# Routing one-hots with pairs of token tiles innermost: one change to a four-block network on one NeuronCore

## The chip, the cores and the metric

The kernel runs on one core of a Trainium2 chip. A core has a matrix engine (TensorE, in the profile PE, with its weight loads as PEld), a vector engine (VectorE, DVE), an activation engine (ScalarE, ACT), a general engine (GpSimd, POOL) and an engine that here only issues DMAs (SyncE, SP). They share the on-chip memory SBUF (128 partitions); TensorE writes to PSUM. Each engine works through its own instructions in order and waits on semaphores for the others. The metric is the device time of one execution in microseconds; the median of several executions counts.

## The reference

The network takes 32 sequences of 256 tokens with 256 features and adds four residual blocks: modulated projection and cosine attention, adapter with attention and a mixture of experts, a second modulated projection with a feature-map attention, and embeddings with a butterfly feed-forward part. The change lies in the mixture of experts, cut here to what matters (T = 8192 tokens, 8 experts, C = 2048 places in each):

```python
logits = x @ wr
top1 = argmax(softmax(logits)); top2 = argmax(logits without top1)
loc1 = cumsum(m1, axis=0) - 1                      # m1, m2: one-hots of top1, top2
loc2 = cumsum(m2, axis=0) - 1 + m1.sum(0)
s1, s2 = loc1[tok, top1], loc2[tok, top2]          # C where the place is past the end
buf[top1, s1] = x; buf[top2, s2] = x               # tokens to places
h = relu(einsum('ecd,edf->ecf', buf, w1) + b1)
y = (einsum('ecf,efd->ecd', h, w2) + b2) * 0.8
out = g1 * y[top1, s1] + g2 * y[top2, s2]          # g: gates
```

To gather the tokens of an expert, the kernel needs the inverse of (expert, place): for each of the 8 x 2048 = 16384 places, the number of the token that sits there.

## The kernel before

The program has two stages, each planned as a whole. The first ("attention stage") runs 32 sequences through both attentions, up to the routing logits `L_all`; the second starts with routing, and goes on with the experts, the butterflies (products of weight matrices on VectorE), and the last two blocks.

**How the order is set.** Work is written as Python generators, `Part`s, which yield an engine and an estimated length before they emit instructions. The function `side_by_side` (L88) is a planner: it keeps a time for each engine, and lets the part go next that can start first. The order in which it emits is the order in each engine's queue on the chip. Buffers come from rings (`ring`, `get`, `back`): a part that wants a buffer of a ring whose turns are all taken waits in the plan too. Thus a different estimate, or a buffer from another ring, can change the written order of everything planned in the same stage. In the attention stage the ring `hp` has 3 buffers of 8 KB a partition, which the first attention's head softmax (L490 to L543) uses for its products; the ring `sh` has 12 of 2 KB. A ring `sc` with one buffer carries the attention scores from TensorE (L716) to ScalarE's exponential (L725, `pt`) in chunks, 8 a sequence.

**Constants.** The part `numbers` (L377) is planned with the attention stage, last in its list, and starts with `yield None, 300.0`, a delay in the plan. It makes the tables that routing needs: `i8b` (the numbers 0 to 127, each repeated), `prow` (the partition's number), `ttb` (the token tile's number), and masks. Its first temporary, `io`, is a buffer of the ring `hp`; the turn is taken when the part is first called, which is before the delay has passed.

**Routing** (L1042). Tokens lie as 64 tiles (NT) of 128 partitions. For each choice k (first, second) VectorE finds the expert (`m`), TensorE counts with a triangular matrix (`loc`, L1090 to L1100) the tokens before each one, and VectorE makes from that a slot number, expert times 2048 plus place, split into `hi` (slot / 128, NHI = 128 values) and `lo` (slot mod 128). The inverse is then computed by products of one-hots. For 8 tiles at a time (AT1), and both choices, that is 16 groups:

- VectorE makes `o1` (L1158: is hi equal to h, for 128 values h and 8 tiles), `ol` (L1161: is lo equal to l, for 128 values l) and the first half of `oh` (L1164: `o1` times the tile's number). All are bf16 with 1024 elements a partition. These three are planned as one step, `DVE2`[...].
- ScalarE makes the second half of `oh` (L1144: `o1` times the partition's number, `prow`).
- TensorE multiplies, for each tile i, `ol[:, :, i]` as weights with `oh[:, :, :, i]` as moving operand (L1135: 128 x 128 by 128 x 256), and sums all 128 products in `tps`: the tile's number and the partition's number of the token at each slot.

In each of these tiles the token tile i is the innermost index, of 8. What one product reads, of weights or of the moving operand, therefore lies 8 bf16 elements, 16 bytes, apart.

After the last product VectorE copies (`tf`, L1172) and combines (`tok`, L1173). GpSimd gathers the experts' tokens by `tok` (L1314), and the expert blocks start: transposes, `bh` (L1358), `by` (L1373), scatter (L1281). The butterflies' VectorE instructions (L1415 to L1421) are planned beside all this. In L1415 and L1419 one operand is a coefficient of a 2 x 2 matrix, taken out of a tile of f32 quadruples.

Of the kernel before, what the change touches and what calls it, by code (L numbers as in the profile page):

```python
# [15 lines left out]
I32 = mybir.dt.int32  # L16
AF = mybir.ActivationFunctionType
ALU = mybir.AluOpType
# [4 lines left out]
P = 128  # L23
# [9 lines left out]
PE, DVE, ACT, POOL, SP = "PE", "DVE", "ACT", "POOL", "SP"  # L33
# [3 lines left out]
BF = mybir.dt.bfloat16  # L37
# [129 lines left out]
def network(ctx: ExitStack, tc: tile.TileContext, a: dict, out: bass.AP):  # L167
    nc = tc.nc
# [5 lines left out]
    NHI = NSL // P  # L174
# [4 lines left out]
    cst = ctx.enter_context(tc.tile_pool(name="cst", bufs=1))  # L179
# [92 lines left out]
    def get(r, name, shape=None, dtype=F):  # L272

        pool, own, turns = rings[r]
        yield turns
        return pool.tile(shape or own, dtype, name=name, tag=r)

    def back(r):
        return "back", rings[r][2]
# [43 lines left out]
    with tc.tile_pool(name="sp", bufs=2) as sp, tc.tile_pool(name="spp", bufs=2, space=PSUM) as spp:  # L323
        wT["c"] = load_w(sp, "cwT", D)
        for l in ("k", "o", "c"):
# [5 lines left out]
            for m in range(2):  # L331
                nc.scalar.activation(
                    sty[l][:, m, :], ps[:, m, :], AF.Identity, bias=col(l + "aff", m),
                    scale=1.0 / math.sqrt(P) if l == "c" else 1.0,
# [18 lines left out]
        for n, o, w in (("dgb", 0, 2 * HID), ("ugb", 2 * HID, 2 * D)):  # L353
            g = sp.tile([P, w], F, name=n)
# [8 lines left out]
    SLAB = P // NE  # L363
    NSB = -(-NT // SLAB)
    AT1 = 8
    i8b = cst.tile([P, P, AT1], BF, name="i8b")
    prow = cst.tile([P, 1], F, name="prow")
    none = cst.tile([P, 1], F, name="none")
    place = cst.tile([P, CAP // P], F, name="place")
    ttb = cst.tile([P, NT], BF, name="ttb")  # L370
# [5 lines left out]

    def numbers():  # L377
        yield None, 300.0
        io = yield from get("hp", "io", [P, P, AT1], I32)
        yield POOL, 1.5  # L380
        nc.gpsimd.iota(io, [[1, P], [0, AT1]], base=0, channel_multiplier=0)
        yield ACT, 1.1
        nc.scalar.copy(i8b, io)
        yield DVE, 0.2
        nc.vector.tensor_scalar(rev, io[:, :NE, 0], -1.0, float(NE), ALU.mult, ALU.add)
        yield back("hp")
        io = yield from get("sh", "io", [P, 2, P], I32)
        yield POOL, 0.3
        nc.gpsimd.iota(io[:, 0, :NT], [[1, NT]], base=0, channel_multiplier=0)
        nc.gpsimd.iota(io[:, 1, :1], [[1, 1]], base=0, channel_multiplier=1)  # L390
        yield ACT, 0.5
        nc.scalar.copy(ttb, io[:, 0, :NT])
        nc.scalar.copy(prow, io[:, 1, :1])
        nc.scalar.activation(none, io[:, 1, :1], AF.Copy, bias=float(T))

        yield POOL, 1.0
        nc.gpsimd.memset(oneb, 1.0)
        nc.gpsimd.affine_select(
            utb, oneb.to_broadcast([P, P]), [[1, P]], ALU.is_ge, 0.0, base=0, channel_multiplier=-1
        )  # L400
        nc.gpsimd.iota(io[:, 0, :NE], [[-1, NE]], base=P, channel_multiplier=1)
        yield DVE, 0.4
        nc.vector.tensor_single_scalar(io[:, 0, :NE], io[:, 0, :NE], NE - 1, ALU.bitwise_and)
        nc.vector.tensor_scalar(e8b, io[:, 0, :NE], 0.0, None, ALU.is_equal)
        nc.gpsimd.iota(io[:, 1, : CAP // P], [[P, CAP // P]], base=0, channel_multiplier=1)
        yield ACT, 0.3
        nc.scalar.copy(place, io[:, 1, : CAP // P])
        yield back("sh")

        for n in range(NSB):  # L410
            yield POOL, 1.2
            nc.gpsimd.affine_select(
                before[:, n, :], e8b.unsqueeze(1).to_broadcast(W3),
                [[NE, NT], [1, NE]], ALU.is_gt, 0.0, base=-P * n, channel_multiplier=-1,
            )
# [548 lines left out]
    with tc.manual_schedule():  # L964
        side_by_side([*(Part(sequence(b, False)) for b in range(B)), Part(numbers())])
# [76 lines left out]
    def routing():  # L1042
# [28 lines left out]
        v_, hi_, lo_, cnt = [], [], [], []  # L1071
        for k in range(2):
# [5 lines left out]
            for n in range(NSB):  # L1078
                w = min(SLAB, NT - n * SLAB) * NE
# [4 lines left out]
            for n in range(NSB):  # L1084
                w = min(SLAB, NT - n * SLAB) * NE
# [5 lines left out]
            for n in range(NSB):  # L1091
                w = min(SLAB, NT - n * SLAB) * NE
# [4 lines left out]
            if k == 1:  # L1097
                for n in range(NSB):
                    w = min(SLAB, NT - n * SLAB) * NE
# [29 lines left out]
        tps = yield from get("mm", "tps", [P, 2, NHI])  # L1129
        last = None  # L1130

        def product(ol, oh, n, w):
            yield PE, 0.12 * w
            for i in range(w):
                nc.tensor.matmul(  # L1135
                    tps.rearrange("p a h -> p (a h)"), ol[:, :, i], oh[:, :, :, i].rearrange("p a h -> p (a h)"),
                    start=(n == 0 and i == 0), stop=(n == 2 * NT - w and i == w - 1),
                )
            yield back("sh")
            yield back("big")  # L1140

        def by_place(ol, oh, o1, n, w, before):
            yield ACT, 1.1
            nc.scalar.activation(oh[:, 1, :, :], o1, AF.Copy, scale=prow)  # L1144
            yield back("sh")
            if before is not None:
                yield "join", before
            yield from product(ol, oh, n, w)

        for k in range(2):  # L1150
            for t0 in range(0, NT, AT1):
                w = min(AT1, NT - t0)
                ol = yield from get("sh", "ol", [P, P, w], BF)
                o1 = yield from get("sh", "o1", [P, NHI, w], BF)
                oh = yield from get("big", "oh", [P, 2, NHI, w], BF)
                OB = [P, P, w]
                yield DVE2, 2.1
                nc.vector.tensor_tensor(  # L1158
                    o1, i8b[:, :NHI, :w], hi_[k][:, t0 : t0 + w].unsqueeze(1).to_broadcast([P, NHI, w]), ALU.is_equal
                )  # L1160
                nc.vector.tensor_tensor(  # L1161
                    ol, i8b[:, :, :w], lo_[k][:, t0 : t0 + w].unsqueeze(1).to_broadcast(OB), ALU.is_equal
                )
                nc.vector.tensor_tensor(  # L1164
                    oh[:, 0, :, :], o1, ttb[:, t0 : t0 + w].unsqueeze(1).to_broadcast([P, NHI, w]), ALU.mult
                )
                last = Part(by_place(ol, oh, o1, k * NT + t0, w, last))
                yield last
        yield "join", last
# [675 lines left out]
    def answer_out(b, begin, before):  # L1845
# [163 lines left out]
        yield "back", lanes_d  # L2009

    routed = Part(routing())
    loads, blocks = [], []
    for e in range(NE):
        w = {}
# [138 lines left out]
```

## Time and profile before

| | |
|---|---|
| median of 3 runs | 3989.45 us (3988.71 to 3994.0) |
| the profiled execution | 3993.62 us |
| its span | 3991.9 us |
| PE busy | 3627.3 us, 91% |
| weight loads | 2607.7 us, 65% |
| VectorE busy | 2471.0 us, 62% |
| ScalarE busy | 1787.2 us, 45% |
| GpSimd busy | 1979.5 us, 50% |
| first one-hot to `tok` | 1853.5 to 1914.6 us |

In the profile an instruction group reads: line, engine, operation, output<-input by the program's names, partitions x elements and type, count. Busy matmul time is pipelined time; a matmul's duration includes its drain, so that the time from one to the next is the busy time divided by the count. A wait line reads: who waited, for whom, microseconds in total, times, longest. The stage times in the busy-time view show the attention stage until about 1830 us, routing until about 1915 us, the experts with the butterflies until about 2850 us, then the last blocks. The granted TensorE clock is 0.50 of the full one from 1850 to 1915 us, and 1.00 from 1940 us on.

### The profile page before, as it was taken

Reading aid. Unit: us, or ns where it says so; the run is one execution under the profiler, and the core shown is the slowest. Engines: PE = TensorE matmul, PEld = TensorE weight load, DVE = VectorE, ACT = ScalarE, POOL = GpSimd, SP = SyncE. Lnnn points to the kernel's source line nnn. Section 1 sums busy time; section 2 is a strip of 40 time slices with the busy share of each in tenths; the row PEclk is TensorE's granted clock in tenths of the full one; section 3 lists DMA queues with packets and bytes.
Section 4 is the critical chain, followed back from the end, with each engine's and each line's share of the span. In section 5 each row is a group of like instructions: output and inputs, shape, how many; then the busy total and the mean of one; then the engine's idle time right before and its main releaser. Section 6 shows DMA issues by size and latency. Waiting matters only on the chain. (4 is left out here: it accounts for less than half of the span.)

```text
span 3991.9 us, 55591 instructions
## 1 busy us (share of the span) xinstructions
PE 3627.3 (91%) x21868; PEld 2607.7 (65%) x21869; DVE 2471.0 (62%) x3951; ACT 1787.2 (45%) x2682; POOL 1979.5 (50%) x1959
## 2 busy tenths in 40 slices
PE   2689898899999999887999999999898999999999
PEld 2356556566666666552566666666686888888888
DVE  6886898898999999625766452000236464565654
ACT  1367666667777777662222222222222333333333
POOL 4554445545555555420644656554215455565653
PEclk7699999999999999995899999999998999999999
DMA  1001000000000000002233433322242323232331
GB/s 63 5 16 32 22 24 15 26 26 26 26 26 26 27 28 26 23 18 90 74 99 91 106 88 85 62 47 48 67 157 77 104 83 104 88 116 87 100 102 43
DMA packets 134368, 237.17 MB, mean 59 GB/s; under 512 B 19249, under 2 KB 80817, under 8 KB 131538
## 3 DMA queue, kind: packets, MB, share of 16 engines
q0 software_dynamic: 48128, 100.77, 10.4%
q1 hardware_dynamic: 85826, 132.25, 9.9%
q8 instruction: 174, 2.85, 0.3%
q14 instruction: 96, 0.79, 0.1%
q10 hardware_dynamic: 144, 0.52, 0.0%
HBM read 182.99 MB, written 50.48 MB: 58 GB/s over the span
## 5 line engine op out<-in xcount | busy, mean ns | idle before, releaser
L725 ACT ACTIVATE pt<-sc 128x2048 f32<-128x2048 f32 x256 | 480.7, 1878 | 204.1 <-PE sc L716 202.0
L1373 PE MATMUL by<-w,hid 128*128 128x256 f32 x2048 | 452.7, 379 | 2.5 <-DVE ysb L1379 2.5
L1358 PE MATMUL bh<-ehT,w 128*128 128x512 f32 x1024 | 452.3, 595 | 1.5 <-ACT ehT L1327 1.5
L1347 ACT ACTIVATE hid<-bh,cols 128x512 f32<-128x512 f32 x256 | 174.8, 688 | 593.1 <-PE bh L1358 548.2
L1373 PEld LDWEIGHTS by<-w,hid 128*128 128x128 f32 x2048 | 386.5, 190 | 66.3 <-issue 13.9
L210 POOL TENSOR_TENSOR n<-n,negh 128x32 f32<-128x32 f32 x64 | 374.1, 5846 | 5.3
L1281 POOL DMA_INDIRECT rrows<-ysb,row x128 | 223.3, 1745 | 260.5 <-DMA rrows<-ysb,row 139.6
L698 PE MATMUL av<-pt,vaug 128*32 128x256 f32 x4096 | 292.0, 405 | 58.7 <-ACT pt L725 56.5
L1358 PEld LDWEIGHTS bh<-ehT,w 128*128 128x128 f32 x1024 | 194.9, 191 | 222.1 <-issue 215.9
L1379 DVE TENSOR_TENSOR ysb<-by,b 128x512 f32<-128x512 f32 x64 | 44.0, 688 | 454.4 <-PE by L1373 333.3
L716 PE MATMUL sc<-qT,kT 32*128 32x256 f32 x4096 | 306.1, 414 | 19.9 <-ACT pt L725 18.7
L539 DVE TENSOR_TENSOR hprod<-hprod 128x1024 f32<-128x1024 f32 (+2 forms) x384 | 317.0, 825 | 7.1
L531 DVE TENSOR_TENSOR hprod<-hex,kk 128x2048 f32<-128x2048 f32 x128 | 298.5, 2332 | 0.0
L716 PEld LDWEIGHTS sc<-qT,kT 32*128 32x128 f32 x4096 | 192.4, 192 | 131.4 <-issue 66.2
L1314 POOL DMA_INDIRECT xg<-h2buf,tok x128 | 150.3, 1174 | 211.5 <-DVE tok L1173 90.3
L1983 PE MATMUL dh<-zT,w_eff 128*128 128x256 f32 x1024 | 238.8, 383 | 5.7 <-DVE zT L1960 5.7
L698 PEld LDWEIGHTS av<-pt,vaug 128*32 128x32 f32 x4096 | 110.6, 113 | 188.1 <-ACT pt L725 86.3
L1997 PE MATMUL do<-w_con,gT 128*128 128x256 f32 x1024 | 231.7, 380 | 0.0
L1983 PEld LDWEIGHTS dh<-zT,w_eff 128*128 128x128 f32 x1024 | 191.2, 192 | 30.7 <-DVE zT L1960 6.9
L1997 PEld LDWEIGHTS do<-w_con,gT 128*128 128x128 f32 x1024 | 193.4, 191 | 25.4
L503 POOL COPY hex<-hex 128x30 f32<-128x30 f32 (+6 forms) x224 | 53.2, 237 | 308.8 <-ACT hex L518 308.8
L208 POOL TENSOR_SCALAR rstd<-mv 128x2 f32<-128x2 f32 x160 | 44.0, 275 | 317.8 <-DVE mv L307 309.9
(612 smaller groups left out, 7585.6 us busy)
## 6 DMA issues: line engine op xcount, KB each, us to landing
w<-in_w SPq DMA_DIRECT2D x16, 1024.0 KB
x<-rrows SPq DMA_DIRECT2D x64, 256.0 KB
bfw<-in_upw SPq DMA_DIRECT2D x10, 1024.0 KB
bfw<-in_dnw SPq DMA_DIRECT2D x10, 1024.0 KB
xT<-in_xT SPq DMA_DIRECT2D x32, 256.0 KB
x<-in_x SPq DMA_DIRECT2D x32, 256.0 KB
h2buf<-xh SPq DMA_DIRECT2D x32, 256.0 KB
ytbuf<-yT SPq DMA_DIRECT2D x32, 256.0 KB
```

Of the source, the lines that this page charges most:

```text
L210: nc.gpsimd.tensor_tensor(o, o, negh[:p].to_broadcast([p, n]), ALU.pow)
L531: nc.vector.tensor_tensor(pr.rearrange("p j (h d) -> p j h d", d=DH), e[:, t, j0 : j0 + 8, :].unsqueeze(3).to_broadcast([P, 8, H, DH]), wi ...
L539: nc.vector.tensor_tensor(pr[:, :n], pr[:, :n], pr[:, n : 2 * n], ALU.add)
L698: nc.tensor.matmul(av[32 * i : 32 * i + 32, c % 2, :], va[:, kc, 4 * c + i, :], pt[:, i, kc, :], start=(kc == 0), stop=(kc == 1),)
L716: nc.tensor.matmul(sc[:, i, kc, :], kT[r, m, kc * P : (kc + 1) * P], qT[r, e, m, :], start=True, stop=nm is None,)
L725: nc.scalar.activation(pt, sc, AF.Exp, scale=1.0 / math.sqrt(DH))
L1281: nc.gpsimd.indirect_dma_start(rrows[:, :], bass.IndirectOffsetOnAxis(ap=row[:, j0 + t : j0 + t + 1], axis=0), y[:, t, :], None, compute_o ...
L1347: nc.scalar.activation(o, ps, AF.Relu, bias=bcol)
L1358: nc.tensor.matmul(ps, w["w1"][:, c, f * P : (f + 1) * P], hT[c], start=(c == 0), stop=(c == 1))
L1373: nc.tensor.matmul(ps[:, t, :], hid[f // 4][:, f % 4, (t0 + t) * P : (t0 + t + 1) * P], w["w2"][:, f, :], start=(f == 0), stop=(f == 7),)
L1983: nc.tensor.matmul(ps[:, g, :], w_eff[:, c, f * P : (f + 1) * P], zT[:, c, :], start=(c == 0), stop=(c == 1))
L1997: nc.tensor.matmul(ps[:, t, :], gT[:, f, t * P : (t + 1) * P], w_con[:, f, :], start=(f == 0), stop=(f == 7))
```

## The change

The one-hots get a new layout. Instead of the 8 tiles of a group innermost, pairs of tiles are innermost, and the group's four pairs are the outermost index: `ol` is [pair, l, 2], `o1` is [pair, h, 2], `oh` is [pair, half, h, 2]. A product reads `ol[:, i // 2, :, i % 2]`: its elements lie 2 bf16 elements, 4 bytes, apart. The elementwise operations on VectorE and ScalarE compute the same values for as many elements; their operands are views with a pair index, in which `hi`, `lo` and `ttb` are repeated over the 128 values (`each`) and the numbers over the pairs (`numbers_`).

`i8b` now repeats each number twice instead of eight times, and is made from a smaller `io`, which is taken from the ring `sh` instead of `hp`. Three of the planner's estimates change with it: the iota, its copy, and a product (0.15 for 0.12).

```diff
-    i8b = cst.tile([P, P, AT1], BF, name="i8b")
+    i8b = cst.tile([P, P, 2], BF, name="i8b")
...
-        io = yield from get("hp", "io", [P, P, AT1], I32)
-        yield POOL, 1.5
-        nc.gpsimd.iota(io, [[1, P], [0, AT1]], base=0, channel_multiplier=0)
-        yield ACT, 1.1
+        io = yield from get("sh", "io", [P, P, 2], I32)
+        yield POOL, 0.5
+        nc.gpsimd.iota(io, [[1, P], [0, 2]], base=0, channel_multiplier=0)
+        yield ACT, 0.4
         nc.scalar.copy(i8b, io)
...
-        yield back("hp")
+        yield back("sh")
...
-            yield PE, 0.12 * w
+            yield PE, 0.15 * w
             for i in range(w):
                 nc.tensor.matmul(
-                    tps.rearrange("p a h -> p (a h)"), ol[:, :, i], oh[:, :, :, i].rearrange("p a h -> p (a h)"),
+                    tps.rearrange("p a h -> p (a h)"), ol[:, i // 2, :, i % 2],
+                    oh[:, i // 2, :, :, i % 2].rearrange("p a h -> p (a h)"),
...
-            nc.scalar.activation(oh[:, 1, :, :], o1, AF.Copy, scale=prow)
+            nc.scalar.activation(oh[:, :, 1, :, :], o1, AF.Copy, scale=prow)
...
-                ol = yield from get("sh", "ol", [P, P, w], BF)
-                o1 = yield from get("sh", "o1", [P, NHI, w], BF)
-                oh = yield from get("big", "oh", [P, 2, NHI, w], BF)
-                OB = [P, P, w]
+                ol = yield from get("sh", "ol", [P, w // 2, P, 2], BF)
+                o1 = yield from get("sh", "o1", [P, w // 2, NHI, 2], BF)
+                oh = yield from get("big", "oh", [P, w // 2, 2, NHI, 2], BF)
+                def each(v, n):
+                    return v[:, t0 : t0 + w].rearrange("p (g i) -> p g i", i=2).unsqueeze(2).to_broadcast([P, w // 2, n, 2])
+                numbers_ = i8b.unsqueeze(1).to_broadcast([P, w // 2, P, 2])
                 yield DVE2, 2.1
-                nc.vector.tensor_tensor(
-                    o1, i8b[:, :NHI, :w], hi_[k][:, t0 : t0 + w].unsqueeze(1).to_broadcast([P, NHI, w]), ALU.is_equal
-                )
-                nc.vector.tensor_tensor(
-                    ol, i8b[:, :, :w], lo_[k][:, t0 : t0 + w].unsqueeze(1).to_broadcast(OB), ALU.is_equal
-                )
-                nc.vector.tensor_tensor(
-                    oh[:, 0, :, :], o1, ttb[:, t0 : t0 + w].unsqueeze(1).to_broadcast([P, NHI, w]), ALU.mult
-                )
+                nc.vector.tensor_tensor(o1, numbers_[:, :, :NHI, :], each(hi_[k], NHI), ALU.is_equal)
+                nc.vector.tensor_tensor(ol, numbers_, each(lo_[k], P), ALU.is_equal)
+                nc.vector.tensor_tensor(oh[:, :, 0, :, :], o1, each(ttb, NHI), ALU.mult)
```

## The prediction

> **What bounds the kernel now.** I read first the page's list of engines (PE busy 91% of a span of 3991.9 us, VectorE 62%), then the waits around the changed lines, which lie near 1850 us, where attention and experts meet.
>
> The waits in the window 1850 to 1930 us (engine, line waited for, us in total, times, longest):
>
> ```profile
> POOL xg L1314 <- DVE tok L1173: 90.3, 1, 90.3
> ...
> DVE tf L1172 <- PE tps L1135: 14.6, 1, 14.6
> DVE oh L1164 <- PE tps L1135: 13.6, 8, 1.8
> ```
>
> GpSimd, which gathers the experts' tokens, stands still until `tok`; `tok` waits for the products' last one, and VectorE waits for products to free one-hots. So here nothing overlaps: what this stage loses or gains, the end loses or gains.
>
> The instructions that write or read `tps` and `ol`:
>
> ```profile
> L1135 PE MATMUL tps<-oh,ol x128: 622/638/644, 1855.5 to 1913.6; 128*128 128x256 bf16 x128
> ...
> L1161 DVE TENSOR_TENSOR ol<-i8b,lo x16: 680/682/686, 1854.1 to 1893.6; 128x1024 bf16<-128x1024 bf16 x16
> ```
>
> The groups by form, TensorE, 1840 to 1916 us (busy us, mean ns):
>
> ```profile
> L1135 PE MATMUL tps<-oh,ol 128*128 128x256 bf16 x128 | 58.8, 638 | 4.7 <-ACT oh L1144 4.7
> L1093 PE MATMUL loc<-before,cnt 128*128 128x512 bf16 x8 | 3.8, 628 | 5.7 <-DVE cnt L1086 5.7
> ```
>
> 128 products in 58.8 us are 0.459 us each for 256 columns, 1.79 ns a column. The neighbours at L1093, bf16 at the same granted clock (0.50), take (timeline: 0.427 us from one weight load to the next) 0.83 ns a column over 512 columns. They read their moving operand without gaps, the products one element in every 16 bytes. So more than half of a product is the reading, not the arithmetic. VectorE shows the same elsewhere: L1415 (512 f32 elements, one input in steps of 16 bytes) means 1086 ns, L1417 (no such step) 680 to 700.
>
> The timeline of the first group:
>
> ```profile
> 1853.49 0.69 DVE L1158 TENSOR_TENSOR o<-i8b,hi 128x1024 bf16<-128x1024 bf16 x1
> 1854.09 0.68 DVE L1161 TENSOR_TENSOR ol<-i8b,lo 128x1024 bf16<-128x1024 bf16 x1
> ...
> 1854.69 0.69 DVE L1164 TENSOR_TENSOR oh<-o,ttb 128x1024 bf16<-128x1024 bf16 x1
> 1855.30 0.68 DVE L1158 TENSOR_TENSOR o<-i8b,hi 128x1024 bf16<-128x1024 bf16 x1
> ```
>
> VectorE starts one of these every 0.602 us when nothing holds it: 1.81 us a group, where TensorE needs 8 x 0.459 = 3.67. TensorE bounds the stage.
>
> [...]
>
> **The change part by part.** Sums go against the profiled execution, 3993.62 us (its span, and 1.7 us around it); it is 4.2 us over the median of 3989.45, which I take as a fixed offset.
>
> *The products (128 matmuls).* Removed: the 16-byte step. Lower bound: 0.213 us at the low clock (half of L1093's 0.427), about 0.11 at the full one. Upper bound from the trace: f32 operands also advance a word per column, and L1373 (256 columns) takes 452.7/2048 = 0.221 us. I take 0.213: 1.71 us a group, just under VectorE's 1.81, so that VectorE becomes the bound and the clock stops mattering. If the weight load (146 ns mean) no longer hides, a product costs up to 0.36 us.
>
> *The one-hots (48 VectorE instructions).* Same count, elements and type; rows of 2 instead of 8, and the output of the third in four pieces. Lower bound 0.602 us each; upper, without pairs, 1.14: today's 512 pairs take as long as 512 f32 elements (0.68 us), and from 512 to 2048 f32 elements (L490, 2.28 us) each adds 1.04 ns, so 512 more add 0.53. In the butterflies' second step (1942 to 1959 us) rows are of two f32 elements, and L1417 still takes 0.68 to 0.70: short rows alone cost nothing there. I take 0.602.
>
> *The new length.* VectorE from 1853.5: 48 x 0.602 = 28.9, to 1882.4. ScalarE's half (1.15 us a group, period 1.81) trails each group's first instruction; group 16's products start at 1855.5 + 15 x 1.81 = 1882.6 and end at 1882.6 + 8 x 0.213 + 0.2 (drain, 0.638 less 0.459) = 1884.5. But three L1415 of the butterflies (3.08 us) stand in VectorE's order ahead of `tf`, as before. They were covered by the wait for TensorE; now they end at 1885.5, and `tf` starts then. It started at 1914.31: 28.8 us less. Their operands are there: the DMA view is empty from about 1860 us.
>
> *After `tok`.* The order on TensorE, GpSimd, ScalarE and VectorE from routing on is the same in both kernels, so the gathers and all behind move up whole. The planner's 0.15 for 0.12 moves no instruction there. I expect no new collision: the experts' first weights have landed by 1860.
>
> *`i8b` and `io` (a quarter the size).* Iota 1412 ns and cast 1052 ns lose about three quarters, in a stretch where GpSimd is half idle and ScalarE's queue isn't the bound: nothing.
>
> *The borrowed buffer.* `io` took one of three `hp` buffers from the plan's beginning until about 363 us; now one of twelve `sh`. So head softmax has three `hp` from the start, and the written order of the whole attention stage (to 1830 us) differs from VectorE's 31st instruction on. Weighing each instruction in that order with its mean duration in the trace, the first head softmax ends after 41 us of VectorE work instead of 44, the last after 1494 in both, and the last five sequences' ends come after 244, 251, 254, 256 of 256 attention chunks before, and 244, 247, 252, 256 after (the fifth from the end: 235, now 236). Work is the same, only its neighbours change. Gain: up to 3 us at the start and one chunk less (about 6.0 us, one `pt` to the next near 1810) behind the last head softmax. Loss: the last four chunks run alone instead of two, about 2 to 4 us each against shared ones. I take 0, from -15 to +20: VectorE idles 156 us in the first 800 and 138 in the last 234 of the stage, single waits reach 21 us, and an order can move one or two of those.
>
> Sum: 3993.6 - 28.8 + 0 = 3964.8 for such an execution, 3960.7 for the median.
>
> **The rivals.**
> *Products still bind ([...]loads exposed).* At 0.30 us each: 128 x 0.30 = 38.4, from 1855.5 to 1894.1, 20.2 us less: 3969. For it: weight loads of 146 ns; against: L1373's 0.221 us with a load of 190 ns hidden.
> *The rows of two cost VectorE its pairs, so the change doesn't do what it says.* 48 x 1.14 = 54.7, plus 3.1: `tf` at 1911.3, 3 us less: 3986.[...]
> *Slower: the attention stage's new order costs more than routing gives.* Place: VectorE's wait at L559 for GpSimd's power function L210 (5.5 us for each of 64 norms, one queue, waited for 57.0 us in 28 cases). An order in which norms come in pairs makes the second wait for the first. It decides from 28.8/64 = 0.45 us more per norm; 0.58 is measurably slower. At 0.7 more: 44.8 - 28.8 = +16, 4005. For it: 28 of 64 already wait; against: the same count, and the same work between marks within some us.
>
> **How the numbers follow.** VectorE-bound routing, order worth little: 0.74, 3949 to 3976 with the order's bounds cut to the likely. Products bind: 0.10 (3969). Pairs lost: 0.08 (3986, either side by order). Order loses: 0.08 (4005). 0.2% is 8 us, about what a measurement of this kernel tells from no change. Faster: the first two and a fourth of the third, 0.86, less 0.04 for an order beyond its bound inside them: 0.82; within: 0.09; slower: 0.09. The range from 3942 (routing's 29 and the order's best) to 3980 (29 less the order's worst) leaves out most of the last two cases.
>
> **What would show it.** Right: 48 one-hot instructions near 0.68 us; VectorE's wait for `tps` gone but for a us or two; one-hots to `tok` in 32 us instead of 61; routing's start within 15 us of 1834. The products' own duration may fall to 0.3 to 0.45 with their drain; what counts is that a group takes no more than 1.81. Wrong: one-hots at 1.2 us; a weight load every 0.3 us with VectorE still waiting; or the first routing instruction 20 us late, with the loss in the L559 or L749 waits before it.

## The result and the profile after

| | before | after |
|---|---|---|
| median of 4 runs each | 3989.08 us (3988.0 to 3994.0) | 3944.32 us (3942.77 to 3951.41) |
| profiled execution / its span | 3993.62 / 3991.9 us | 3951.41 / 3949.7 us |
| routing's first instruction (`mx`, L1059) | 1834.3 | 1816.3 |
| `tok` (L1173) | 1914.6 | 1867.7 |
| from `tok` to the end | 2077.3 | 2082.0 |

The ratio is 0.9889, with a 95% interval of 0.9872 to 0.9906: 44.8 us, or 1.1%, faster. Laid out along the span, the difference of -42.2 us is -18.0 before routing starts, -29.0 in routing (80.3 us from `mx` to `tok` before, 51.3 after), and +4.8 behind `tok`. The forecast was 3961, from 3942 to 3980, with 0.82 for faster. The time lies within the range, but 17 us under the forecast. Routing's part is as forecast; the difference is what was gained ahead of routing, less the few us behind it.

The waits of the kernel after, from 1835 to 1930 us (engine, line waited for, us in total, times, longest):

```profile
POOL xg L1314 <- DVE tok L1173: 61.2, 1, 61.2
...
PEld L1135 <- DVE oh L1166: 19.0, 16, 5.5
...
PE tps L1135 <- ACT oh L1145: 12.8, 12, 4.7
```

GpSimd's wait for `tok` is 29.1 us shorter (it was 90.3). VectorE's two waits for TensorE, 14.6 and 13.6 us before, are gone; now it is TensorE that waits, for one-hots.

The products, and the instruction that reads their sum, in the kernel after (duration in ns, smallest, median and largest; first and last start):

```profile
L1135 PE MATMUL tps<-oh,ol x128: 273/274/415, 1837.5 to 1865.4; 128*128 128x256 bf16 x128
L1172 DVE COPY tf<-tps x1: 287/287/287, 1867.3 to 1867.3; 128x128 f32<-128x128 f32 x1
```

The timeline of TensorE in the middle of routing, after (start, length, count, idle time before):

```profile
1850.12 1.07 PE L1135 MATMUL tps<-oh,ol 128*128 128x256 bf16 x8 [0.74 <-ACT oh L1145]
1851.92 1.07 PE L1135 MATMUL tps<-oh,ol 128*128 128x256 bf16 x8 [0.74 <-ACT oh L1145]
```

A group of 8 takes 1.07 us; without the last one's duration of 0.274 that is 7 steps of 0.114 us, where a product took 0.459 before. From the start of one group to the next it is 1.81 us (the period), and for 0.74 of it TensorE is idle. Who sets the period is seen in VectorE's timeline, at the beginning and the end of the one-hots:

```profile
1835.47 0.68 DVE L1164 TENSOR_TENSOR o<-i8b,hi 128x1024 bf16<-128x1024 bf16 x1
1836.07 0.69 DVE L1165 TENSOR_TENSOR ol<-i8b,lo 128x1024 bf16<-128x1024 bf16 x1
1836.67 0.68 DVE L1166 TENSOR_TENSOR oh<-o,ttb 128x1024 bf16<-128x1024 bf16 x1
...
1863.77 0.68 DVE L1166 TENSOR_TENSOR oh<-o,ttb 128x1024 bf16<-128x1024 bf16 x1
1864.37 3.05 DVE L1415 TENSOR_TENSOR bft<-w_eff,bfw 128x512 f32<-128x512 f32 x3
1867.33 0.29 DVE L1172 COPY tf<-tps 128x128 f32<-128x128 f32 x1
1867.65 0.29 DVE L1173 SCALAR_TENSOR_TENSOR tok<-tps,tf 128x128 int32<-128x128 f32 x1
```

A one-hot still starts every 0.60 us, rows of two and all; 48 of them fill 1835.47 to 1864.37 without a gap. Then come the three butterfly instructions, and `tf` follows them directly. The last product, started at 1865.4, has long ended.

The first instruction of routing, from the views of `mx` (before, then after):

```profile
L1059 DVE TENSOR_REDUCE mx<-L_all x1: 685/685/685, 1834.3 to 1834.3; 128x64 f32<-128x512 f32 x1
```

```profile
L1059 DVE TENSOR_REDUCE mx<-L_all x1: 685/685/685, 1816.3 to 1816.3; 128x64 f32<-128x512 f32 x1
```

Of the work ahead of it only `io` and `i8b`, which are smaller now, and the two instructions that make them differ. So 18 us have come from something else: either from the order in which the attention stage is now written, or by chance from one execution to the next.

### The profile page after: what moved, and what is told of

It is laid out like the page before. It is cut to its first block, busy times and chain, and to the rows that moved or that the text cites. A ratio compares the mean times of both kernels' runs of the same rounds, so it can differ in the third digit from the quotient of the medians.

```text
span 3949.7 us, 55584 instructions
## 1 busy us (share of the span) xinstructions
PE 3586.3 (91%) x21869; PEld 2603.4 (66%) x21869; DVE 2459.5 (62%) x3951; ACT 1786.6 (45%) x2682; POOL 1983.5 (50%) x1959
## 5 line engine op out<-in xcount | busy, mean ns | idle before, releaser
L1373 PE MATMUL by<-w,hid 128*128 128x256 f32 x2048 | 454.4, 380 | 3.9 <-DVE ysb L1379 3.9
L1373 PEld LDWEIGHTS by<-w,hid 128*128 128x128 f32 x2048 | 387.6, 191 | 68.2 <-issue 13.6
```

The source lines that it names most:

```text
L1373: nc.tensor.matmul(ps[:, t, :], hid[f // 4][:, f % 4, (t0 + t) * P : (t0 + t + 1) * P], w["w2"][:, f, :], start=(f == 0), stop=(f == 7),)
```

## The experiments

Two questions are to be settled. What in the layout made the products slow, and what limits them now? And where do the 18 us ahead of routing come from? For the second one I had these theories:

- **A**: the head softmax has its third `hp` buffer from the start, since `io` no longer holds it. The buffer is the cause.
- **B**: the written order as a whole decides how well the engines' work interlocks in the attention stage. Any edit that shifts the planner's choices draws another order, and this change drew a good one.

A third theory, **C**, was added for the last orders: the numbers are made early or late in start-up, and that is what costs or saves.

In all tables below a time of `mx` or `tok` is that in the profiled execution. The kernels of the first pair and of the last were run four times each. The eight in between were run once each, so a difference of a few us between their times says nothing.

### One half at a time: the layout, and the order

The first kernel has the new layout, but takes `io` from the ring `hp` with the old estimates, so that every engine's written order is that of before (against the kernel after):

```diff
-        io = yield from get("sh", "io", [P, P, 2], I32)
-        yield POOL, 0.5
+        io = yield from get("hp", "io", [P, P, 2], I32)
+        yield POOL, 1.5
...
-        yield ACT, 0.4
+        yield ACT, 1.1
...
-        yield back("sh")
+        yield back("hp")
```

> The new one-hot layout, with io in a buffer of hp and the old estimates, so that every engine's order is that of the kernel before. Theory (two independent parts: layout 29 us in routing, order 18 us in the attention stage): routing's first instruction at 1834 us as before, tok 29 us earlier, 3960 us, ratio 0.9927. Rival (the attention stage's gain comes from the smaller iota and cast themselves): 3944 us with the attention stage 18 us shorter.

The second has the layout of before (tiles innermost, 16-byte steps), with `io` in the ring `sh`, and so the written order of after. Its `i8b` is as wide as before (against the kernel before):

```diff
-        io = yield from get("hp", "io", [P, P, AT1], I32)
-        yield POOL, 1.5
-        nc.gpsimd.iota(io, [[1, P], [0, AT1]], base=0, channel_multiplier=0)
-        yield ACT, 1.1
-        nc.scalar.copy(i8b, io)
+        io = yield from get("sh", "io", [P, P, 2], I32)
+        yield POOL, 0.5
+        nc.gpsimd.iota(io, [[1, P], [0, 2]], base=0, channel_multiplier=0)
+        yield ACT, 0.4
+        nc.scalar.copy(
+            i8b.rearrange("p l (r i) -> p l r i", i=2), io.unsqueeze(2).to_broadcast([P, P, AT1 // 2, 2])
+        )
...
-        yield back("hp")
+        yield back("sh")
```

> The old layout (16-byte steps), with io taken from sh and the new estimates, so that every engine's order is that of the changed kernel. Theory of two independent parts: routing's first instruction at 1816 us, one-hots to tok 61 us as before, 3971 us, ratio 0.9955. Rival (a later stage gives the attention stage's gain back): 3985 us or more.

| | median | ratio to before, 95% | `mx` | `mx` to `tok` |
|---|---|---|---|---|
| before, same chip | 3994.93 us | | 1834.3 | 80.3 us |
| layout alone | 3965.62 | 0.9931 (0.9915 to 0.9948) | 1834.1 | 51.3 |
| order alone | 3973.94 | 0.9944 (0.9927 to 0.9961) | 1815.1 | 80.3 |

(The row of before has its median on this chip; its `mx` and `tok` are those of the profile shown at the beginning.)

The first line of the view of `mx` in the kernel with the layout alone, and then in that with the order alone, whose lines are shifted by two:

```profile
L1059 DVE TENSOR_REDUCE mx<-L_all x1: 687/687/687, 1834.1 to 1834.1; 128x64 f32<-128x512 f32 x1
```

```profile
L1061 DVE TENSOR_REDUCE mx<-L_all x1: 687/687/687, 1815.1 to 1815.1; 128x64 f32<-128x512 f32 x1
```

By the medians, the layout gives 29.3 us (0.69% by the ratio), and the profile has its gain in routing. The order gives 21.0 us (0.56% by the ratio), and the profile has its gain ahead of routing. Together that is 50.3. A later pair of runs, at the end of this part, gives 49.3 for the whole change, and the first one gave 44.8: within a few us the halves add up. The smaller iota and its copy aren't what gains ahead of routing, since the kernel with the layout alone has them too, and starts routing when the one before does. Chance is no explanation of the 18 us either. All eight executions profiled with the written order of after have `mx` between 1810.0 and 1816.3, whatever their layout; the two with the order of before have it at 1834.1 and 1834.3.

### What in the order: the buffer, the estimates, or anything

The next kernel keeps the new layout and the new estimates, but takes `io` from `hp`, as before:

```diff
-        io = yield from get("sh", "io", [P, P, 2], I32)
+        io = yield from get("hp", "io", [P, P, 2], I32)
...
-        yield back("sh")
+        yield back("hp")
```

> The new layout and the new estimates, but io in a buffer of hp as before. Theory A (what shortens the attention stage is that head softmax has its third hp buffer in the first 300 us): the 16th sequence's L938 at 1084 us as before, routing's start at 1834 +- 6, 3960 us. Theory B (any reshuffling of the order moves the stage this much, hp has no part in it): the 16th L938 and routing's start off by 10 us or more from before, either way.

And this one has the old estimates, but asks for `hp` only after the part's delay, so that the third buffer is free in start-up:

```diff
         yield None, 300.0
-        io = yield from get("sh", "io", [P, P, 2], I32)
-        yield POOL, 0.5
+        yield POOL, 0.0
+        io = yield from get("hp", "io", [P, P, 2], I32)
+        yield POOL, 1.5
```

(with 1.1 for ScalarE, and `back("hp")`, as in the kernel with the layout alone).

> The new layout and the old estimates, io in a buffer of hp, but asked for only when the plan has passed the 300 us, so that hp has three buffers until then and two for a while after it. Theory A: the 16th sequence's L938 at 1057 us within 10, as in the changed kernel, 3944 us within 12 (the end of the stage may differ). Theory B: anywhere, 1060 to 1100.

The first came to 3962.79 us, with `mx` at 1828.1; the second to 4006.03, with `mx` at 1873.6. Neither theory had all its marks. With the third buffer taken, as before, and the new estimates, the 16th sequence came 44 us earlier than before (1040.9 against 1084.5), where A had expected no change. Of this lead 6 us were left at `mx`, about what A allowed, and the time was near A's 3960; B had expected 10 or more. With the third buffer free in start-up the 16th sequence came at 1049.9, within A's 10 us of 1057 and earlier than B had allowed; but `mx` came 39 us later than before, and the time missed A's 3944 by 62. So an early lead doesn't need the free buffer, and a free buffer in start-up did not bring an early `mx`. The second kernel is no clean test of the buffer alone, though, since it takes one of `hp` after start-up, which the kernel after never does.

Two more orders were then drawn from the kernel after, by the delay alone: `yield None, 0.0` and `yield None, 700.0` in the place of 300.0.

> The kernel after, with the part that makes the table of numbers asked for at the start (a delay of 0 in the place of 300 planned us). The same work is done; only the written order of all engines differs, from the first 30 instructions of VectorE on. Theory B (the attention stage's length depends on the whole written order, and what the change did to it was one draw): routing's first instruction moves from 1816 by more than 5 us, in either direction, into the stretch of 1805 to 1875 that the four orders run so far span, with TensorE's wait for VectorE and ScalarE spread over many lines; routing itself stays at 51 us from its first instruction to the token table (52 at most). Theory C (the gain of 18 us comes from the numbers being made early and without the borrowed buffer of the first kind): 1816 or earlier, within 5 us at most on the late side, since here they are made earlier still; about 3944, at most 3950.

> The kernel after, with the part that makes the table of numbers asked for at 700 planned us in the place of 300. Start-up (the first 300 us) then has no such instruction in it, and the written order is the same as after's for longer. Theory B: routing's first instruction moves by more than 5 us, in either direction, within 1805 to 1875. Theory C (the gain comes from the numbers leaving start-up free): 1816 within 5 us. Either way routing takes 51 us from its first instruction to the token table, and the time is 3944 plus the move of the first instruction, within 8 us.

They came to 3983.61 us (`mx` at 1858.9) and 4012.75 us (`mx` at 1886.2). Both lose against 1816 by far more than 5 us, so C falls. A falls with it: both take `io` from `sh`, so that all three buffers of `hp` are free from the start, as in the kernel after, and both start routing later than the kernel before. The second is beyond even the stretch of 1805 to 1875 that I gave to B. The part from `mx` to `tok` is 51.3 us in both, as expected. The time of the second was to be 3944 plus the move of `mx`, which is 4014; it is within 2 us of that. The first lines of the views of `mx` in the four kernels, in the order in which they were told:

```profile
L1059 DVE TENSOR_REDUCE mx<-L_all x1: 687/687/687, 1828.1 to 1828.1; 128x64 f32<-128x512 f32 x1
L1060 DVE TENSOR_REDUCE mx<-L_all x1: 687/687/687, 1873.6 to 1873.6; 128x64 f32<-128x512 f32 x1
L1059 DVE TENSOR_REDUCE mx<-L_all x1: 685/685/685, 1858.9 to 1858.9; 128x64 f32<-128x512 f32 x1
L1059 DVE TENSOR_REDUCE mx<-L_all x1: 685/685/685, 1886.2 to 1886.2; 128x64 f32<-128x512 f32 x1
```

Here are the six orders, by when the 16th and the 26th sequence's last sum in the attention stage (L938) starts. All of them compute the same:

| order | 16th | 26th | from 16th to 26th | from 26th to `mx` | `mx` |
|---|---|---|---|---|---|
| before | 1084.5 | 1578.8 | 494.3 | 255.5 | 1834.3 |
| after | 1057.5 | 1552.2 | 494.7 | 264.1 | 1816.3 |
| new estimates, `io` in `hp` | 1040.9 | 1550.6 | 509.7 | 277.5 | 1828.1 |
| `hp` asked for late | 1049.9 | 1568.9 | 519.0 | 304.7 | 1873.6 |
| delay 0 | 1061.9 | 1602.4 | 540.5 | 256.5 | 1858.9 |
| delay 700 | 1090.1 | 1589.7 | 499.6 | 296.5 | 1886.2 |

Before and after run alike in the middle. The order of after leads by 27 us at the 16th sequence, keeps this to the 26th, and gives 9 of it back at the end. The other orders lose in the middle (up to 46 us), or behind it (up to 49 us). What this looks like on the engines is seen in the busy times from 900 to 1550 us, before and then with the delay of 700 (us, then busy time with the count of instructions of TensorE, weight loads, VectorE, ScalarE and GpSimd; granted clock, DMA share, GB/s):

```profile
900.00:1550.00 650.00, 610.16 (x5297) 404.94 (x5298) 587.47 (x857) 471.26 (x668) 371.98 (x384) 0.99 0.09 27
```

```profile
900.00:1550.00 650.00, 577.93 (x4792) 382.59 (x4791) 552.39 (x782) 430.05 (x606) 327.58 (x350) 0.96 0.07 23
```

In the same 650 us TensorE issues 4792 matmuls instead of 5297, and every engine is idle for longer. Its granted clock is lower too, 0.96 against 0.99; whether that is a part of the loss or follows from the idle time was not separated. I found no single wait that holds the loss. My rival had named one, VectorE's at L559 for GpSimd's power function. Over the first 1900 us, before and then with the delay of 700:

```profile
DVE qk L559 <- POOL n L210: 57.0, 28, 5.3
```

```profile
DVE qk L559 <- POOL n L210: 46.5, 29, 5.7
```

The order that loses 52 us waits there less than the one of before; with the delay of 0 it is 33.4 us. So it is established that the written order moved `mx`, and that the six orders differ by 70 us, where executions of one order differ by up to 6. Which of its features makes an order good I haven't found: that stays open.

### What made the products slow: which operand, which step

The following kernels all have the order of after. Each of the next differences shows how the products read; the lines that make the tiles change to match. In two of them only one operand of the products is read in steps of 16 bytes, the other in steps of 4. First the weights:

```diff
-                    tps.rearrange("p a h -> p (a h)"), ol[:, i // 2, :, i % 2],
+                    tps.rearrange("p a h -> p (a h)"), ol[:, :, i],
                     oh[:, i // 2, :, :, i % 2].rearrange("p a h -> p (a h)"),
...
-                ol = yield from get("sh", "ol", [P, w // 2, P, 2], BF)
+                ol = yield from get("sh", "ol", [P, P, w], BF)
...
```

> The changed kernel with only the weights (ol) in the old layout, read in steps of 16 bytes; the moving operand in steps of 4. If the moving operand alone made the products slow: a product every 0.13 to 0.24 us (128 weight columns at 1.79 ns are 0.229 us, beside the matmul), routing 32 us, 3944 us. If the weights did: a product every 0.46 us, routing 61 us, 3973 us.

Then the moving operand:

```diff
                     tps.rearrange("p a h -> p (a h)"), ol[:, i // 2, :, i % 2],
-                    oh[:, i // 2, :, :, i % 2].rearrange("p a h -> p (a h)"),
+                    oh[:, :, :, i].rearrange("p a h -> p (a h)"),
...
-                o1 = yield from get("sh", "o1", [P, w // 2, NHI, 2], BF)
-                oh = yield from get("big", "oh", [P, w // 2, 2, NHI, 2], BF)
+                o1 = yield from get("sh", "o1", [P, NHI, w], BF)
+                oh = yield from get("big", "oh", [P, 2, NHI, w], BF)
...
```

> The changed kernel with only the moving operand (o1, oh) in the old layout, read in steps of 16 bytes; the weights in steps of 4. If the moving operand made the products slow: a product every 0.459 us, routing 61 us, 3973 us. If the weights did: 0.13 to 0.24 us, routing 32 us, 3944 us.

In the next, four tiles are innermost, and both operands are read in steps of 8 bytes. Two outcomes were weighed: 8 bytes cost no more than 4 (1.07 us for a group of 8 after, by 8), or half as much as 16 (half of 0.459 us):

```diff
-                    tps.rearrange("p a h -> p (a h)"), ol[:, i // 2, :, i % 2],
-                    oh[:, i // 2, :, :, i % 2].rearrange("p a h -> p (a h)"),
+                    tps.rearrange("p a h -> p (a h)"), ol[:, i // 4, :, i % 4],
+                    oh[:, i // 4, :, :, i % 4].rearrange("p a h -> p (a h)"),
...
```

> The changed kernel with four tiles innermost, so that products read in steps of 8 bytes[...].[...] a product every 0.134 us at the full clock, as with 4 bytes, and the same time, 3944 us.[...] 0.9 ns a column, a product every 0.23 us, a group in 1.83 us against VectorE's 1.81, and still no more than 2 us longer.

In the last, the tiles are outermost: the products read both operands without gaps, and on VectorE `hi`, `lo` and `ttb` are repeated along the innermost index. Two outcomes were weighed: this slows VectorE's instructions to the prediction's upper bound, or it doesn't:

```diff
-                    tps.rearrange("p a h -> p (a h)"), ol[:, i // 2, :, i % 2],
-                    oh[:, i // 2, :, :, i % 2].rearrange("p a h -> p (a h)"),
+                    tps.rearrange("p a h -> p (a h)"), ol[:, i, :],
+                    oh[:, i, :, :].rearrange("p a h -> p (a h)"),
...
-                    return v[:, t0 : t0 + w].rearrange("p (g i) -> p g i", i=2).unsqueeze(2).to_broadcast([P, w // 2, n, 2])
+                    return v[:, t0 : t0 + w].unsqueeze(2).to_broadcast([P, w, n])
...
```

> The changed kernel with the tiles outermost, so that products read without gaps, and one VectorE operand of each one-hot is repeated with an innermost step of zero.[...] the 48 one-hot instructions start every 1.13 us instead of 0.602, tok 26 us later, 3970 us. If a step of zero keeps the pairs: 0.602 us and 3944 us, since VectorE sets the stage[...].

The groups by form from 1805 to 1925 us (busy us, mean ns, then idle time ahead and who ended it). Weights in 16-byte steps:

```profile
L1137 PE MATMUL tps<-oh,ol 128*128 128x256 bf16 x128 | 23.1, 337 | 17.1 <-ACT oh L1147 14.8 <-DVE oh L1168 2.3
...
L1166 DVE TENSOR_TENSOR o<-i8b,hi 128x1024 bf16<-128x1024 bf16 x16 | 17.5, 1092 | 0.0
```

The moving operand in 16-byte steps:

```profile
L1137 PE MATMUL tps<-oh,ol 128*128 128x256 bf16 x128 | 58.2, 633 | 5.0 <-DVE oh L1168 5.0
...
L1167 DVE TENSOR_TENSOR ol<-i8b,lo 128x1024 bf16<-128x1024 bf16 x16 | 16.8, 1051 | 0.0
L1137 PEld LDWEIGHTS <-ol 128*128 128x128 bf16 x128 | 16.1, 126 | 47.0 <-issue 39.8 <-DVE oh L1168 6.5 <-DVE ol L1167 0.7
```

Both operands in 8-byte steps:

```profile
L1137 PE MATMUL tps<-oh,ol 128*128 128x256 bf16 x128 | 29.7, 410 | 4.6 <-ACT oh L1147 4.6
```

Both operands without gaps:

```profile
L1135 PE MATMUL tps<-oh,ol 128*128 128x256 bf16 x128 | 30.2, 418 | 29.0 <-DVE oh L1166 29.0
L1164 DVE TENSOR_TENSOR o<-i8b,hi 128x1024 bf16<-128x1024 bf16 x16 | 19.4, 1215 | 0.0
```

| step of moving operand / weights | one product at a clock of 0.50 | at 1.00 | `mx` to `tok` | time (before on the same chip 3987.75) |
|---|---|---|---|---|
| 16 / 16 bytes (order alone) | 0.459 us | | 80.3 us | (another chip) |
| 16 / 4 | 0.455 | | 80.0 | 3966.43 us |
| 8 / 8 | 0.229 | 0.231 us | 51.4 | 3936.16 |
| 4 / 4 (after) | 0.21 | 0.114 | 51.3 | (another chip) |
| 4 / 16 | 0.21 | 0.117 | 57.9 | 3939.91 |
| 2 / 2 | 0.21 | | 76.9 | 3958.38 |

The four times on this chip came 4 to 12 us under those expected. In all four the part from `tok` to the end took 2068.1 to 2070.4 us, against 2082.0 in the first profile of after; the time from `mx` to `tok` is the better measure of a layout here.

The first two times of a product are busy time by 128. The others come from the timeline: a group that runs without a gap, less the last one's duration, by the number of steps. For the groups of 8 that is 1.07 less 0.274, 1.10 less 0.282 and, at a clock of 0.50, some 1.86 to 1.89 less 0.415 to 0.421 us, by 7.

Where a row has two clocks, the kernel itself had both in routing. The busy times of the kernel with 8-byte steps, and then of the kernel after (columns as above; the last three are granted clock, DMA share, GB/s):

```profile
1836.20:1839.80 3.60, 3.60 (x16) 1.82 (x17) 3.60 (x7) 2.30 (x2) 0.00 (x0) 0.50 0.84 338
1839.80:1865.80 26.00, 26.00 (x119) 13.22 (x119) 26.00 (x42) 14.95 (x13) 0.00 (x0) 1.00 0.02 6
```

```profile
1837.40:1841.00 3.60, 3.55 (x16) 2.01 (x16) 3.60 (x7) 2.30 (x2) 0.00 (x0) 0.50 0.98 398
1841.00:1865.80 24.80, 15.19 (x125) 10.58 (x124) 24.80 (x41) 14.93 (x13) 0.00 (x0) 1.00 0.01 4
```

The timeline of the products in these stretches: with 8-byte steps the first 16 and the other 112, and the first 8 of the kernel after:

```profile
1836.16 3.84 PE L1137 MATMUL tps<-oh,ol 128*128 128x256 bf16 x16 [4.65 <-ACT oh L1147]
1839.83 26.00 PE L1137 MATMUL tps<-oh,ol 128*128 128x256 bf16 x112
```

```profile
1837.45 1.86 PE L1135 MATMUL tps<-oh,ol 128*128 128x256 bf16 x8 [4.65 <-ACT oh L1145]
```

The moving operand is what made the products slow. With its step alone at 16 bytes, nearly the whole time of before is back. With the weights' step alone at 16 bytes, a product takes 0.117 us at the full clock, and its weight load stays hidden, though longer than in the kernel after (151 and 101 ns on the mean, over both clocks):

```profile
L1137 PEld LDWEIGHTS <-ol 128*128 128x128 bf16 x128 | 16.6, 151 | 24.0 <-DVE oh L1168 22.0
```

```profile
L1135 PEld LDWEIGHTS <-ol 128*128 128x128 bf16 x128 | 12.2, 101 | 21.3 <-DVE oh L1166 19.0
```

What a step cost depended on the clock. With 8 bytes a product took the same at half the clock (0.229 us: 3.84 less 0.41, by 15) as at the full one (0.231: 26.00 less 0.41, by 111), so here the reading set its time and not the clock. With 4 bytes it took 0.21 us at half the clock and 0.114 at the full one, so there the clock set it. At half the clock, 2 and 4 bytes were alike (0.21), 8 cost about a tenth more (0.229), and 16 took twice as long as 8 (0.455). At the full clock, 8 took twice as long as 4 (0.231 against 0.114). In the two rows where the reading set the time, TensorE took in about 9 bytes of *extent*, gaps counted in, per ns and partition (256 columns x 16 bytes / 455 ns, x 8 / 231). The 0.114 us of 4-byte steps lies near half of the gapless operand's 0.21 at half the clock, so by this estimate 4 bytes are nearly as good as no gap at the full clock too. The gapless operand did not run at the full clock here, and the 16-byte step neither. That a full clock would leave the 16-byte step as slow as it left the 8-byte one is an estimate too, and not shown.

The busy times in routing with the moving operand in 16-byte steps, and with both operands in 8-byte steps:

```profile
1836.00:1893.00 57.00, 57.00 (x127) 15.96 (x126) 35.83 (x48) 17.24 (x15) 0.00 (x0) 0.50 0.05 20
```

```profile
1836.20:1865.80 29.60, 29.60 (x134) 15.05 (x135) 29.60 (x48) 17.26 (x15) 0.00 (x0) 0.94 0.12 46
```

TensorE is busy without a gap in both. It was granted 0.50 of its clock throughout the first. In the second, 0.94 is the mean of 0.50 for 3.6 us and 1.00 after them. Why the clock rose in the one and not in the other these runs don't show.

VectorE bounded routing in all rows but those with a 16-byte moving operand (with that step alone it waited 7.7 us for products ahead of `oh`, and 14.4 ahead of `tf`); with 8-byte steps both engines worked without a gap (26.00 us of 26.00). So 8-byte steps gave routing the same length as 4-byte ones (51.4 and 51.3 us): TensorE's 8 x 0.231 = 1.85 us a group almost equal VectorE's 1.81. And the gapless layout, for TensorE no better than 4-byte steps at half the clock (0.21 us each), made VectorE slower: 1215 ns an instruction instead of 684, 25.6 us more in routing. This is the loss that the rival "pairs lost" spoke of, which did not come about with rows of two, made to happen. (Its word for 1024 bf16 elements in the time of 512 f32 ones, 682 ns at L1161 and 680 to 700 at L1417 in the kernel before, was pairs; how VectorE comes to that time was not shown.) Its price of 1.14 us from one to the next was about right: 1.14 from the group's period of 3.41 us in the timeline (1846.28 to 1849.68), by three.

In the two mixed kernels one operand of the one-hots lies otherwise too (rows of two, taken from the wide `i8b`, 16 bytes apart), and VectorE takes 1.05 to 1.09 us for these instead of 0.68. This explains the 6.6 us by which routing with 16-byte weights is longer than after: 16 x (1.092 - 0.684) = 6.5.

### Eight-byte steps, timed, beside the kernel after

> Four tiles innermost (steps of 8 bytes) once more, timed against the kernel before, beside the kernel after on the same chip. In the one look at it, routing took 51.4 us from its first instruction to the token table, as in the kernel after (51.35), since VectorE sets both; its 3936 against after's 3944 then came from the part behind the table. Theory (VectorE bounds routing at either step, the rest is spread from run to run): its median within 6 us of the median of after here. Rival (something behind the table is faster with it): 6 to 10 us under after.

> The kernel after, unchanged, as the yardstick for four tiles innermost on the same chip: 3944 us, within 7; routing's first instruction at 1816 within 5 us, since the written order is the same.

Four tiles innermost: 3933.01 us (3928.67 to 3935.35), ratio to before 0.9867 (0.9851 to 0.9884). After, unchanged: 3937.52 us (3935.72 to 3938.94), ratio 0.9877 (0.9860 to 0.9893). Before, on the same chip: 3986.81 us. The 4.5 us between the two are within the 6 that were expected, and the intervals of the ratios overlap widely, so no gain is taken as shown. It is not excluded either: the slowest of the four runs with 8-byte steps (3935.35) is a little faster than the fastest of after (3935.72). If there is a gain, the profiles have most of it behind the table, since routing is the same and starts within 1 us. The part from `tok` to the end takes 2064.6 us in the one and 2071.7 in the other; over all fourteen profiled executions it is 2064.6 to 2082.0, and after itself had 2082.0 and 2071.7. The 4.8 us that the first comparison seemed to lose there lie within this spread. No experiment gave a version that is shown to beat the kernel after.

## Why the prediction was right, and where it was not

**The products: right, and conservatively sized.** I took 0.213 us, with 0.11 at the full clock as the lower bound. That a 4-byte step would cost no more than no gap was my estimate: no product of 2-byte elements was read so in the kernel before. It was 0.21 in the first two groups, at a clock of 0.50, and 0.114 in the others, at 1.00; I hadn't counted on the clock to rise. This gave nothing more, as the prediction said it wouldn't: VectorE had become the bound, and TensorE's gain turned into 0.74 us of idle time a group. The upper bound, by the 0.221 us of L1373's f32 products, had the reading of a word per column as its reason. That isn't what made those slow: with a 4-byte step bf16 products took half of it (0.114 us) at the same clock of 1.00.

**The one-hots: right.** 48 in 28.9 us, at 0.602 from one to the next. That rows of two would take no longer than rows of eight was my estimate; they took 684 ns an instruction against 682.

**The new length: right in mechanism and size.** Forecast: `tf` 28.8 us earlier, because three L1415 end only then. Measured from `mx`: 80.0 us to `tf` before, 51.0 after, 29.0 less; with the layout alone the whole time fell by 29.3. Without the three L1415 in VectorE's order, `tf` could have started once the last product had ended, up to 1.7 us earlier (1865.4 + 0.27 against 1867.3).

**After `tok`: right.** Everything moved up whole, within the spread of this part.

**The borrowed buffer: the term that was mis-sized.** The step saw that the written order of the attention stage changes, and priced it at 0, from -15 to +20. It was -18.0 in the profile, and -21.0 us in the timed run of the order alone, outside that range. The reason given, "work is the same, only its neighbours change", is true and not enough: with the same work, six orders put `mx` anywhere from 1816.3 to 1886.2, -18 to +52 against before. The weighing that I did, VectorE's instructions by mean duration, looks at one engine at a time, and can't see how the engines wait for each other: in each of these orders every engine has the same work. A price from it was a guess within too narrow bounds, and so the sign of the result owes something to luck, to the order that was drawn: with that of the delay of 700 the same layout came to 4012.75 us, beside 3994.29 for before (one run of each).

**The range: held by slack.** Its lower end was to be routing's 29 us and the order's best: 3989.45 - 28.8 - 15 = 3945.6, not 3942. The measured 3944.3 lies below that sum, as it must with an order's term beyond its best case. That it lies within the stated range owes to the 4 us that the sum doesn't give.

**The rivals.** "Products still bind" and "pairs lost" did not happen. "The attention stage's new order costs more than routing gives" did not happen with this change, but the stage had the room for it: it is what happened in the kernels with `hp` asked for late and with a delay of 700. Its place was wrong: with the delay of 700 the wait at L559 did not grow.

**What would show it.** All the signs of a right forecast were there (one-hots at 0.68, no wait of VectorE for `tps`, 32.2 us from the first one-hot to `tok`) but one: routing's start was to lie within 15 us of 1834, and it lay 18.0 away.

## What to carry to other kernels

Look at the step in which TensorE's products read their moving operand, and at what the layout does to the engine that makes it. Here a product took 0.455 us with 16-byte steps, 0.229 with 8-byte ones and 0.21 with 4-byte ones or no gap, at half the clock; at the full one it took 0.231 with 8 and 0.114 with 4 (eight cost routing nothing, since VectorE's part was as long). Among these layouts the one to choose was one whose one-hots VectorE made no slower than before (rows of two and four took 684 and 678 ns an instruction, an operand repeated along the innermost index 1215). The weights' step mattered far less: 0.117 us a product with 16 bytes, 0.114 with 4. Where a planner or pools write the order, look at what an edit to an unimportant temporary (its ring, its estimate, its delay) does to everything planned with it, and take the spread of a few such orders as the uncertainty of any forecast. To know what a layout is worth, run it with the order held as before, and the order with the old layout: here the two added up, 29 and 21 us.

## What the runs showed of the hardware that was not expected

- A matmul of 256 bf16 columns took 0.229 us at half the clock and 0.231 at the full one when its moving operand was read in 8-byte steps: a faster clock gave it nothing. In 4-byte steps it took 0.21 and 0.114, and in 16-byte steps 0.455 at half the clock.
- A step of 16 bytes in the weights cost almost nothing: 0.117 us a product against 0.114 at the full clock, with weight loads of 151 ns instead of 101 hidden behind the products.
- TensorE was granted half its clock throughout 57 us in which its records show it busy without a gap, with a 16-byte step. With an 8-byte step and the same busy share it was granted the full clock after 3.6 us. In these two runs a busy row in the profile did not tell which clock was granted (0.50 and 1.00).
- VectorE took as long for 1024 bf16 elements in rows of two that lie side by side (684 ns) as in rows of eight (682); with one operand's rows 16 bytes apart it took 1051 to 1092 ns, and with an operand repeated along the innermost index 1215 ns.
